# A state-space and MLP block in one kernel: the second tile's first norm moved ahead of the first tile's second norm, with another order at both ends

## The chip, the cores and the metric

The kernel runs on one core of one Trainium2 chip. The metric is the device time of one launch in microseconds (us), the median of several runs. A profile is one execution of the same program, taken by the hardware profiler; its span runs from the first to the last instruction of the program on the core, and its own time is a little longer than the span.

Engines are named as in the profile: PE (TensorE matmul), PEld (its weight loads), DVE (VectorE), ACT (ScalarE), POOL (GpSimd) and SP (SyncE, which here only issues DMAs). Each engine takes its instructions in the order of the program.

## What is computed

The input `u` has 16 sequences of 1024 steps with 256 channels; `c` has one conditioning row for each sequence. Everything is float32. Cut to what matters, with `mod` split into six rows of 256 for each sequence:

```python
mod = (silu(c) @ wmod).reshape(16, 6, 1, 256)
sa, ca, ga, sb, cb, gb = (mod[:, i] for i in range(6))
ga, gb = sign(ga) * maximum(abs(ga), 0.25), sign(gb) * maximum(abs(gb), 0.25)

h  = layernorm(x) * (1 + ca) + sa              # first norm, "a"
Bu = (h @ W_B.T + b_B) * exp(log_dt)
xs = scan(state = A_bar * state + Bu)          # along the sequence
x  = x + ga * (xs @ W_C.T + b_C + h @ W_D.T + b_D)

h  = layernorm(x) * (1 + cb) + sb              # second norm, "b"
y  = square(relu(h @ W_fc.T)) @ W_proj.T       # 256 -> 1024 -> 256
x  = x + gb * (spikes of y in 5 steps) / 5
```

The number of spikes depends on `y` alone and rises at five levels, so the kernel counts how many levels `y` exceeds.

## The kernel before

**Tiles.** The 16 x 1024 rows are cut into 32 tiles of 512 rows (`TILES`, `TT`); tiles 2b and 2b+1 are the two halves of sequence b, and the scan of an odd tile goes on from the state of the even one. A tile lies in SBUF either with channels on the partitions (two blocks of 128, `KD`) and 512 rows along the free dimension, or with rows on the partitions (four blocks of 128, `SUB`), which is where a norm's moments are taken.

**Products.** A float32 value is split into a high part (rounded to the matmul's fp32r form, by an ACT copy) and a low part (the rest, by a DVE subtraction), and every product is made in three passes: high by high, low weight by high value, high weight by low value (`PASSES`, line 222). So a block of 128 x 128 x 512 costs three matmuls, and every operand needs an ACT step (`..._hi`, `halves`) and a DVE or POOL step (`..._lo`, `halves_lo`).

**One tile's way.** Its names in the profile:

- `moments`, `aggregate`, `root_in_v`, `root`, `newton_v` (lines 243 to 305): the first norm's statistics on DVE (tiles st_a, mv_a, v_a), a square root on ACT (q_a), then five small DVE steps to the scale and the shift (r_a, m_a). `normalise` or `normalise_by` (lines 307 to 328) apply them (xn_a), on ACT alone or on the engines listed.
- To bring xn_a to channels on the partitions the first tiles use `transpose` (line 384: eight 128 x 128 transposes on PE into pt_a), all later ones `hop` (line 330): a 32 x 32 transpose on DVE (w_a), four DMAs to DRAM (hop_a) and one back (v_a). `scaled_hi`/`scaled_lo`, or `turned_hi`/`turned_lo` after a hop, multiply by 1 + ca and split: h_a.
- `state_input` (line 408): 12 matmuls with W_B into pb. `state_bias` on ACT (bu), `state_scan` on DVE (xs), `state_hi`/`state_lo` (xsp).
- `mix_h` (line 445): 12 matmuls of h_a with W_D into py; `mix_xs` (line 450): 12 of xsp with W_C into the same py. `mix_out` or `mix_out_late` make x1 (in the profile x or x_N), the residual stream; with `mix_out` the input tile x has had a constant added by `residual` before.
- The second norm, the same with b for a, from xm: `transpose_back` (line 395: eight transposes on PE into pm) for tiles 0 and 1, `hop_back` (line 344, hop_x, xm) later.
- `expand` (lines 478 to 503), for each of four pairs of hidden blocks: 12 matmuls into pf, then on ACT relu (a), square (a) and the high copy (hid); `hidden_lo` makes the low half. `contract` (line 516): 12 matmuls for each pair into pp.
- `spike` (line 524): five DVE comparisons (o); `gated` on ACT, `output` on POOL, then the DMA out.

**Order.** The order on each engine is that of the program text: `InOrder` (line 71) keeps it. From tile 2 on `period(t)` (line 871) interleaves the expand and contract steps of tile t with the first norm of tile t+4, the scan of t+3, the mix of t+2 and the second norm of t+1. `first_period` (line 718) and `second_period` (line 821) are written out by hand, as is the front (lines 614 to 716), where modulations, weights and the first tile's chain are made, and `last_tile` (line 548), which works in column halves of 256 rows. `load` and `load_q` (lines 110 to 123) fetch x and xq.

**Buffers that matter.** PSUM: `ps_f` has four buffers, `ps_y` and `ps_p` two each (lines 99 to 101); SBUF: tag "hid" four, "relu" three, "o" four. The raw weights wm1, wm2, ff and fp lie in "hid" buffers until they have been used.

**Small products.** `columns` (line 206) makes one modulation row for all sequences (ps_sa, ps_ca, ps_ga, ps_cb, ps_sb, ps_gb), ps_bb, ps_bd and ps_bf the biases that follow from them. They are float32 matmuls with 16 columns; each is two instructions in the profile. `run_idle` (line 618) multiplies zeros while the first inputs are on their way.

Of the kernel before, what the change touches and what calls it, by code (L numbers as in the profile page):

```python
# [21 lines left out]
F32 = mybir.dt.float32  # L22
# [64 lines left out]
def adaln_kernel(ctx: ExitStack, tc: tile.TileContext, x, xq, w_bT, w_cT, w_dT, w_fcT, w_projT, cols,  # L87
# [38 lines left out]
    Q.dma_start(out=col, in_=cols)  # L126
# [6 lines left out]
    load_q(0)  # L133
    Q.dma_start(out=wm1[:, :, 0:D], in_=wm_v[:, :, 0:D])
    fb, fcm, fd = (work.tile([P, KD, D], F32, tag="relu", name=n, bufs=3) for n in ("fb", "fc", "fd"))
    Q.dma_start(out=fb, in_=w_bT.rearrange("(k p) n -> p k n", p=P))
    Q.dma_start(out=wm1[:, :, D:2 * D], in_=wm_v[:, :, D:2 * D])
# [327 lines left out]
    def residual(t):  # L465

        b = t // 2
        for m in range(KD):
            G.tensor_scalar(xts[t][:, m], xts[t][:, m], gac[:, m, b:b + 1], None, ALU.add)
# [78 lines left out]
    def last_tile(t):  # L548
# [4 lines left out]
        hid = [work.tile([P, 2, 2, TT], F32R, tag="hid", name=f"hid_{t}_{pair}", bufs=HIDB)  # L553
               for pair in range(KF // 2)]

        def expand_half(g, pair):
            a = work.tile([P, 2, half], F32, tag="relu", name=f"a_{t}_{pair}_{g}", bufs=3)
# [9 lines left out]

        acc = ps_p.tile([P, KD, half], F32, tag="ps_p", name=f"pp_{t}_0")
        for pair in range(KF // 2):
            expand_half(0, pair)  # L570
            if pair < 2:
                output(t - 2, (pair, 0))
# [17 lines left out]
        for m, pairs in ((0, (0, 1)), (1, (0, 1)), (0, (2, 3)), (1, (2, 3))):  # L590
# [27 lines left out]
    def run_idle(n):  # L618
        PE.matmul(ps_zero[:, 0:n], lhsT=zero[:, 0:P], rhs=zero[:, 0:n], start=True, stop=True)

    for _ in range(2):
        run_idle(TT)
    silu_c()
    S.activation(sa[:, 0, 0:1], edt, AF.Sqrt)
    ps_sa = columns(wm1, 0, "sa")
    decay(6)
# [3 lines left out]
    root("a0")  # L630
    S.activation(sa, ps_sa, AF.Copy)
    decay(1)
    ps_ca = columns(wm1, 1, "ca")
# [6 lines left out]
    S.activation(wb[:, 0], fb, AF.Identity, scale=edt)  # L640
    S.activation(wd[:, 0], fd, AF.Copy)
    newton_v("a0", lambda: decay(1))
    normalise_by("a0", blocks_of(xqs[0]), (V, S, V, S))
    V.tensor_scalar(s1, ps_ca, 1.0, None, ALU.add)
    V.scalar_tensor_tensor(wb[:, 1], fb, edt, wb[:, 0].bitcast(F32), ALU.mult, ALU.subtract)
    transpose("a0")
    decay(2)
# [3 lines left out]
    scaled_hi("a0", lambda k: pts["a0", k])  # L651
    scaled_lo("a0", lambda k: pts["a0", k])
    V.tensor_tensor(wd[:, 1], fd, wd[:, 0].bitcast(F32), ALU.subtract)
    S.activation(wc[:, 0], fcm, AF.Copy)
    state_input(0)
# [11 lines left out]
    state_scan(0, (1,))  # L667
    state_lo(0, slice(0, 1))
    V.tensor_tensor(wc[:, 1], fcm, wc[:, 0].bitcast(F32), ALU.subtract)
    state_hi(0, slice(1, 2))  # L670
# [4 lines left out]
    state_lo(0, slice(1, 2))  # L675
    mix_xs(0)
    ps_cb = columns(wm2, 1, "cb")
    ps_sb = columns(wm2, 0, "sb")
    mix_out_late(0)
    S.activation(sb, ps_sb, AF.Copy)  # L680
    moments("a1", blocks_of(xqs[1]))
    transpose_back(0, ps_p, "ps_p")
    moments("b0", xms[0])
    aggregate("b0")
    root_in_v("b0")
    root("b0")
    halves(wf, ff, *fc(0))
    newton_v("b0")
    V.tensor_scalar(s2, ps_cb, 1.0, None, ALU.add)
    normalise_by("b0", xms[0], (V, S, V, S))  # L690
    halves_lo(wf, ff, *fc(0), V)
    clipped(columns(wm2, 2, "gb"), gb, sil, 1.0 / STEPS)

    ps_bf = ps_f.tile([P, KF, NB], F32, tag="ps_f", name="ps_bf")

    def shift_f(*blocks):
        for m in blocks:
            for k in range(KD):
                PE.matmul(ps_bf[:, m], lhsT=ff[:, k, m * P:(m + 1) * P], rhs=sb[:, k],
                          start=k == 0, stop=k == KD - 1)  # L700

    shift_f(0, 1, 2, 3, 4, 5, 6)
    transpose("b0")
    shift_f(7)
    halves(wf, ff, *fc(1))
    halves_lo(wf, ff, *fc(1), G)
    scaled_hi("b0", lambda k: pts["b0", k])
# [163 lines left out]
    def period(t):  # L871
# [17 lines left out]
        if one:  # L889
            root(b1)  # L890
# [97 lines left out]
```

## Time and profile before

| | us |
|---|---|
| median of 3 runs | 1006.14 (1005.83 to 1007.24) |
| the profiled execution, its own time | 1003.88 |
| its span | 1002.1 |
| first matmul (zeros) | 1.44 |
| first matmul of tile 0 with 512 columns (pb) | 11.99 |
| first matmul of tile 0's expand (pf) | 34.29 |
| end of the last mix_h in `first_period` | 83.63 |
| end of the last matmul | 995.2 |
| end of the last DVE instruction | 998.81 |

Landing times of the first DMAs, from the DMA view: col (issued by SP at 0.72) 2.46, xq of tile 0 (issued at 1.17) 4.82, the first third of wm1 5.51, fb 6.81, the second third of wm1 7.55, fd 8.29, fc 9.73, xq of tile 1 11.01, wm2 14.24, ff 16.81, fp 22.32.

How to read it: a row of a timeline has the start, the time from the start of the first to the end of the last merged instruction, the engine, the line (all have that of the recording helper, 81, so one goes by tiles), the operation with out<-in, and the number of instructions; in brackets the idle time before and what ended it. Matmuls are pipelined, and one that waits for an operand is shown as busy; whether PE flows is seen from the steps between starts.

### The profile page before, as it was taken

How to read it: one execution, taken by the hardware profiler on the slowest of the kernel's cores; microseconds unless marked ns; L12 is line 12 of the kernel's file. 1: busy time of each engine (PE TensorE's matmuls, PEld its weight loads, DVE VectorE, ACT ScalarE, POOL GpSimd, SP SyncE). 2: the span in 40 equal slices, each digit the busy share in tenths (PEclk: the TensorE clock that was granted, in tenths of full speed). 3: DMA queues.
4: the chain of work that ended last, by engine and by line, in shares of the span. 5: the costliest groups of instructions: out<-in, count | busy, mean ns of one | idle time of the engine just before them, and what ended most of it. 6: DMA issues, size and time to landing. Idle time of an engine off the chain costs nothing.

```text
span 1002.1 us, 13540 instructions
## 1 busy us (share of the span) xinstructions
PE 989.8 (99%) x4468; PEld 819.7 (82%) x4468; DVE 856.0 (85%) x1654; ACT 767.4 (77%) x1157; POOL 288.7 (29%) x317
## 2 busy tenths in 40 slices
PE   8999999999999999999999999999999999999997
PEld 6877778888888888888888888888888888888887
DVE  6788998898888899888889888889888889887775
ACT  4676888778778878777878777878777877876785
POOL 0202232332332232332232332233332233332111
PEclk8899999999999999999999999999999999999999
DMA  7134455555544555545555544554554554453321
GB/s 284 49 121 147 147 155 167 166 154 164 182 133 151 180 157 155 172 140 152 171 163 154 168 136 153 174 168 148 168 152 143 168 168 148 147 161 112 99 70 43
DMA packets 125335, 150.09 MB, mean 150 GB/s; under 512 B 9552, under 2 KB 89424, under 8 KB 125264
## 3 DMA queue, kind: packets, MB, share of 16 engines
q1 hardware_dynamic: 125264, 149.22, 48.7%
q8 instruction: 35, 0.57, 0.2%
q14 instruction: 36, 0.29, 0.1%
HBM read 85.22 MB, written 63.96 MB: 149 GB/s over the span
## 4 chain that ended last, share of the span: by engine, by line
PE 84%; DVE 4%; DMA 2%; ACT 1%; issue 1%; SPq 0%; DVEq 0%
PE pp L81 31%; PE pf L81 31%; PE py L81 15%; PE pb L81 7%; DVE o L81 2%; DMA v_b<-hop_b 1%; DMA hop_b<-w_b 0%; DVE st_b L81 0%; DMA v_a<-hop_a 0%; SPq L81 0%; DVE w_b L81 0%; DVE hid L81 0%; ACT xn_a L81 0%; ACT a L81 0%; ACT h_b L81 0%
## 5 line engine op out<-in xcount | busy, mean ns | idle before, releaser
L81 PE MATMUL pp<-hid,wp 128*128 128x512 f32 (+1 forms) x1584 | 366.9, 383 | 2.0 <-DVE o L81 0.7
L81 PE MATMUL pf<-h_b,wf 128*128 128x512 f32 (+1 forms) x1584 | 365.5, 383 | 0.0
L81 PEld LDWEIGHTS pp<-hid,wp 128*128 128x128 f32 x1584 | 290.3, 188 | 63.4 <-DVE hid L81 2.4
L81 PEld LDWEIGHTS pf<-h_b,wf 128*128 128x128 f32 x1584 | 291.7, 188 | 58.5 <-DVE h_b L81 0.4
L81 ACT ACTIVATE a<-pf,bias_f 128x512 f32<-128x512 f32 (+1 forms) x264 | 169.1, 668 | 156.4 <-PE pf L81 156.2
L81 DVE TENSOR_TENSOR hid<-a,hid 128x1024 fp32r<-128x1024 f32 (+1 forms) x131 | 152.1, 1181 | 93.0 <-ACT hid L81 93.0
L81 POOL TENSOR_TENSOR o<-o,x 128x512 f32<-128x512 f32 x64 | 108.2, 1710 | 298.0 <-ACT o L81 298.0
L81 DVE SCALAR_TENSOR_TENSOR o<-pp,o 128x512 f32<-128x512 f32 (+1 forms) x260 | 177.4, 682 | 7.9
L81 ACT ACTIVATE a<-a 128x1024 f32<-128x1024 f32 (+1 forms) x132 | 136.7, 1036 | 4.2
L81 ACT ACTIVATE hid<-a 128x1024 fp32r<-128x1024 f32 (+1 forms) x132 | 136.7, 1035 | 4.2
L81 POOL TENSOR_SCALAR x<-x,gac 128x512 f32<-128x512 f32 x60 | 93.5, 1568 | 29.2 <-DVE o L81 19.9
L81 POOL TENSOR_SCALAR v_a<-mv_a 128x4 f32<-128x4 f32 x26 | 15.6, 600 | 283.6 <-DVE mv_a L81 283.6
L81 PE MATMUL pb<-h_a,wb 128*128 128x512 f32 x384 | 94.3, 394 | 0.1
L81 PE MATMUL py<-xsp,wc 128*128 128x512 f32 x384 | 92.7, 390 | 0.5 <-ACT xsp L81 0.5
L81 PE MATMUL py<-h_a,wd 128*128 128x512 f32 x384 | 92.4, 389 | 0.0
L81 PEld LDWEIGHTS pb<-h_a,wb 128*128 128x128 f32 x384 | 73.0, 190 | 16.5 <-ACT h_a L81 0.9
L81 PEld LDWEIGHTS py<-xsp,wc 128*128 128x128 f32 x384 | 71.9, 188 | 15.9 <-ACT xsp L81 1.1
L81 PEld LDWEIGHTS py<-h_a,wd 128*128 128x128 f32 x384 | 72.0, 188 | 15.0
L81 ACT ACTIVATE xn_a<-xq,m_a,r_a 128x256 f32<-128x256 f32 x124 | 64.3, 592 | 1.6 <-PE pb L81 1.1
L81 ACT ACTIVATE xn_b<-xm,m_b,r_b 128x256 f32<-128x256 f32 x120 | 61.9, 587 | 1.0 <-DVE m_b L81 1.0
L81 DVE TENSOR_SCALAR o<-pp 128x512 f32<-128x512 f32 (+1 forms) x65 | 44.4, 682 | 13.3 <-PE pp L81 13.1
L81 ACT ACTIVATE o<-o,gb 128x512 f32<-128x512 f32 (+1 forms) x65 | 42.6, 702 | 3.5 <-issue 3.5
(123 smaller groups left out, 839.4 us busy)
## 6 DMA issues: line engine op xcount, KB each, us to landing
xq<-in_xq SPq DMA_DIRECT2D x32, 512.0 KB, 6.7
x<-in_x SPq DMA_DIRECT2D x32, 512.0 KB, 5.1
out<-o SPq DMA_DIRECT2D x63, 256.0 KB, 6.8
hop_a<-w_a SPq DMA_DIRECT2D x120, 128.0 KB, 2.5
v_a<-hop_a SPq DMA_DIRECT2D x30, 512.0 KB, 4.0
hop_x<-w_x SPq DMA_DIRECT2D x120, 128.0 KB, 3.1
xm<-hop_x SPq DMA_DIRECT2D x30, 512.0 KB, 3.2
hop_b<-w_b SPq DMA_DIRECT2D x120, 128.0 KB, 2.5
```

The source lines that it names most:

```text
L81: return self.tc.keep_in_program_order(issue(*args, **kwargs))
```

## The change

The diff touches four places.

1. **Loads.** col is issued by ACT's queue in place of SP's; xq of tile 0 goes first on SP, in two halves; the thirds of wm1 change places (ca's columns before sa's).
2. **Front.** `run_idle` now multiplies zeros in fp32r form, twelve times at first and three times after each of ps_ca and ps_sa. Tile 0's transposes come ahead of ps_bb; the high copy of wd comes after h_a. Tile 1's first norm (moments, aggregate, root, newton, normalise), its transposes, h_a and its W_B products (`state_input(1)`) come ahead of tile 0's second norm. ps_bf is made in two halves, the second one and ps_gb only after tile 0's first expand products, and ps_bf moves to the pool ps_y. The steps of `first_period` stand in another order (tile 1's second norm ahead of tile 3's normalise, among others), and `residual(2)` is done by ACT.
3. **The last periods.** `period` runs to tile 29; in tile 29 newton stands before the second spike, normalise and hop before the next steps, `turned_hi`/`turned_lo` before the last expand, and the last contract is left to the next period. Tile 30 has a period of its own, `period_before_last`.
4. **The last tile.** Its first expand products stand ahead of contract(30, 3), the spikes of tile 30 stand between them, and the last contract runs in another order of pairs.

```diff
-    Q.dma_start(out=col, in_=cols)
+    S.dma_start(out=col, in_=cols)
+    xqs[0] = io.tile([P, SUB, D], F32, tag="xq", name="xq_0", bufs=2)
+    for s in (slice(0, 2), slice(2, 4)):
+        Q.dma_start(out=xqs[0][:, s], in_=xq[0][:, s])
...
-    def residual(t):
+    def residual(t, E=G):
...
+            if E is S:
+                S.activation(xts[t][:, m], xts[t][:, m], AF.Identity, bias=gac[:, m, b:b + 1])
+            else:
+                G.tensor_scalar(xts[t][:, m], xts[t][:, m], gac[:, m, b:b + 1], None, ALU.add)
...
     def last_tile(t):
...
+        expand_half(0, 0)
+        expand_half(0, 1)
+        contract(t - 1, 3)
+        for m in range(KD):
+            output(t - 2, (m, 0))
+        for m in range(KD):
+            spike(t - 1, accs.pop((t - 1, m)), (m, 0))
+            expand_half(0, 2 + m)
         acc = ps_p.tile([P, KD, half], F32, tag="ps_p", name=f"pp_{t}_0")
-        for pair in range(KF // 2):
-            expand_half(0, pair)
-            if pair < 2:
-                output(t - 2, (pair, 0))
...
-        for m, pairs in ((0, (0, 1)), (1, (0, 1)), (0, (2, 3)), (1, (2, 3))):
+        for m, pairs in ((0, (0, 1, 2)), (1, (0,)), (0, (3,)), (1, (1, 2, 3))):
...
     def run_idle(n):
-        PE.matmul(ps_zero[:, 0:n], lhsT=zero[:, 0:P], rhs=zero[:, 0:n], start=True, stop=True)
-
-    for _ in range(2):
-        run_idle(TT)
+        for _ in range(n):
+            PE.matmul(ps_zero, lhsT=zero[:, 0:P].bitcast(F32R), rhs=zero.bitcast(F32R), start=True, stop=True)
+
+    run_idle(12)
     silu_c()
     S.activation(sa[:, 0, 0:1], edt, AF.Sqrt)
+    ps_ca = columns(wm1, 1, "ca")
+    run_idle(3)
     ps_sa = columns(wm1, 0, "sa")
+    run_idle(3)
```

The front from tile 0's statistics on, as it reads after the change (small steps left out):

```python
    normalise_by("a0", blocks_of(xqs[0]), (V, S, V, S))
    S.activation(sa, ps_sa, AF.Copy)
    ...
    transpose("a0")
    decay(4)
    ...
    scaled_hi("a0", lambda k: pts["a0", k])
    scaled_lo("a0", lambda k: pts["a0", k])
    ...
    moments("a1", blocks_of(xqs[1]))
    state_input(0)
    state_bias(0)
    state_scan(0, (0,))
    mix_h(0)
    ...
    state_hi(0, slice(0, 1))
    state_scan(0, (1,))
    aggregate("a1")
    root_in_v("a1")
    root("a1")
    state_hi(0, slice(1, 2))
    V.tensor_tensor(wc[:, 1], fcm, wc[:, 0].bitcast(F32), ALU.subtract)
    state_lo(0, slice(0, 1))
    newton_v("a1")
    state_lo(0, slice(1, 2))
    normalise_by("a1", blocks_of(xqs[1]), (S, S, V, S))
    clipped(ps_ga, ga, gac, 1.0)
    ...
    mix_xs(0)
    transpose("a1")
    ps_cb = columns(wm2, 1, "cb")
    ps_sb = columns(wm2, 0, "sb")
    mix_out_late(0)
    V.tensor_scalar(s2, ps_cb, 1.0, None, ALU.add)
    scaled_hi("a1", lambda k: pts["a1", k])
    S.activation(sb, ps_sb, AF.Copy)
    transpose_back(0, ps_p, "ps_p")
    scaled_lo("a1", lambda k: pts["a1", k])
    moments("b0", xms[0])
    aggregate("b0")
    root_in_v("b0")
    state_input(1)
    state_bias(1, (0,))
    root("b0")
    halves(wf, ff, *fc(0))
    state_bias(1, (1,))
    newton_v("b0")
    normalise_by("b0", xms[0], (V, S, V, S))
    halves_lo(wf, ff, *fc(0), V)
    shift_f(0, 1, 2, 3)
    transpose("b0")
    ...
```

`first_period` after, up to where it reads as before again (three dots mark steps left out):

```python
        r0 = expand_begin(0, 0)
        ...
        r0(0)
        root("a2")
        halves(wf, ff, *fc(2))
        state_scan(1)
        newton_v("a2")
        shift_f(4, 5, 6, 7)
        r0(1)
        halves_lo(wf, ff, *fc(2), V)
        clipped(columns(wm2, 2, "gb"), gb, sil, 1.0 / STEPS)
        residual(2, S)
        r1 = expand_begin(0, 1)
        normalise_by("a2", blocks_of(xqs[2]), (S, V, S, V))
        hop("a2")
        load_q(4)
        r1(0)
        mix_h(1)
        state_hi(1)
        state_lo(1)
        r0(2)
        hidden_lo(0, 0)
        ...
        mix_xs(1)
        r2(0)
        root("a3")
        mix_out_late(1)
        contract(0, 0)
        newton_v("a3")
        turned_hi("a2")
        turned_lo("a2")
        r2(1)
        transpose_back(1, ps_f, "ps_f")
        ...
        r2(2)
        root("b1")
        halves(wf, ff, *fc(3))
        newton_v("b1")
        halves_lo(wf, ff, *fc(3), V)
        contract(0, 1)
        normalise("a3", blocks_of(xqs[3]))
        hop("a3")
        load_q(5)
        state_input(2)
        state_bias(2)
        state_scan(2)
        normalise("b1", xms[1])
        ...
        hidden_lo(0, 2)
        mix_h(2)
        ...
        turned_hi("a3")
        turned_lo("a3")
        r3 = expand_begin(0, 3)
        ...
```

The period of tile 30 (t = 30), new:

```python
    def period_before_last(t):
        b1 = f"b{t + 1}"
        rest = expand_begin(t, 0)
        rest(0)
        ...
        contract(t - 1, 3)
        rest(1)
        normalise(b1, xms[t + 1])
        rest(2)
        spike(t - 1, accs.pop((t - 1, 0)), (0, 0))
        hop(b1)
        for m in range(KD):
            output(t - 2, (m, 0))
        expand(t, 1)
        spike(t - 1, accs.pop((t - 1, 1)), (1, 0))
        hidden_lo(t, 0)
        expand(t, 2)
        hidden_lo(t, 1)
        rest = expand_begin(t, 3)
        rest(0)
        hidden_lo(t, 2)
        rest(1)
        contract(t, 0)
        rest(2)
        contract(t, 1)
        turned_hi(b1)
        turned_lo(b1)
        ...
        hidden_lo(t, 3)
        contract(t, 2)
```

## The prediction

> **What bounds the kernel now.** I read the page first, then the busy time by stretch, then the timelines of PE, DVE and ACT at both ends, and last the step from each matmul's start to the next. PE sets the end, so what counts is where its stream has holes.
>
> ```profile
> PE 989.8 (99%) x4468; PEld 819.7 (82%) x4468; DVE 856.0 (85%) x1654; ACT 767.4 (77%) x1157; POOL 288.7 (29%) x317
> ```
>
> The 99% hides the holes, because a matmul that waits for its operand counts as busy. The steady step shows them: two successive groups of the middle, twelve products of 512 columns each, start 2.72 us apart, 0.227 us per product.
>
> ```profile
> 912.74 2.88 PE L81 MATMUL pb<-h_a,wb 128*128 128x512 f32 x12
> 915.46 2.88 PE L81 MATMUL pp<-hid,wp 128*128 128x512 f32 x12
> ```
>
> Against 0.227 (0.121 for 256 columns, 0.101 for the instructions of small products and transposes) the stream loses 12.5 us from 0 to 36, 2.7 from 36 to 92, 1.9 from 92 to 150, nothing from 150 to 940, and 1.9 between 945 and 970. Only the ends can move.
>
> The stretches (us, then busy time of PE, PEld, DVE, ACT, POOL; granted TensorE clock; DMA) show the front's first cause: the clock is halved twice, once while tile 0's W_B products run and once into its first expand products.
>
> ```profile
> 8.80:15.60 6.80, 6.74 (x23) 5.38 (x24) 4.22 (x13) 3.24 (x7) 0.00 (x0) 0.51 1.03 411
> 15.60:29.30 13.70, 13.70 (x95) 12.47 (x93) 9.85 (x27) 4.40 (x10) 0.00 (x0) 0.99 0.44 158
> 29.30:36.10 6.80, 6.80 (x30) 6.54 (x31) 5.18 (x20) 4.00 (x8) 2.27 (x2) 0.51 0.00 0
> 150.00:940.00 790.00, 790.00 (x3487) 654.36 (x3486) 692.06 (x1288) 620.94 (x920) 249.90 (x280) 1.00 0.52 155
> ```
>
> PE's timeline shows the chain: pb takes 4.68 us instead of 2.72, the eight transposes before it 1.9 instead of 0.8, and from x1 (pm, 25.68) to the first pf (34.29) PE has small products alone.
>
> ```profile
> 10.11 1.95 PE L81 MATMUL pt_a<-ident,xn_a 128*128 128x128 f32 x8
> 11.99 4.84 PE L81 MATMUL pb<-h_a,wb 128*128 128x512 f32 x12
> 16.67 2.90 PE L81 MATMUL py<-h_a,wd 128*128 128x512 f32 x12
> ...
> 21.11 3.03 PE L81 MATMUL py<-xsp,wc 128*128 128x512 f32 x12
> ...
> 25.68 1.07 PE L81 MATMUL pm<-ident,x 128*128 128x128 f32 x8
> ...
> 31.84 1.95 PE L81 MATMUL pt_b<-ident,xn_b 128*128 128x128 f32 x8
> ...
> 34.29 4.01 PE L81 MATMUL pf<-h_b,wf 128*128 128x512 f32 x13
> ```
>
> DVE there: a1's moments stand ahead of b0's.
>
> ```profile
> 24.54 1.36 DVE L81 TENSOR_TENSOR x<-x,x 128x512 f32<-128x512 f32 x2 [1.91 <-ACT x L81]
> 25.81 1.40 DVE L81 BATCH_NORM_STATS2 st_a<-xq 128x6 f32<-128x256 f32 x4
> 27.13 1.41 DVE L81 BATCH_NORM_STATS2 st_b<-pm 128x6 f32<-128x256 f32 x4
> ```
>
> At the end PE's last group starts at 989.29 and stops at 995.2. DVE counts spikes of column half m=0 from 993.87 for 2.2 us, so m=1 starts at 996.05, 0.75 us after PE is done.
>
> ```profile
> 993.87 0.43 DVE L81 TENSOR_SCALAR o<-pp 128x256 f32<-128x256 f32 x1 [1.24 <-PE pp L81]
> ...
> 996.05 0.41 DVE L81 TENSOR_SCALAR o<-pp 128x256 f32<-128x256 f32 x1
> ...
> 998.33 0.48 DVE L81 SCALAR_TENSOR_TENSOR o<-o,gb,x 128x256 f32<-128x256 f32 x1
> ```
>
> **Base of the sum.** The profiled execution took 1003.88 us (span 1002.1 and 1.8 around it), 2.26 below the median 1006.14; I take the saving off the median.
>
> **Tile 0's first norm.** col leaves by ACT's queue, xq0 first on SP in two halves. SP issued xq at 1.17 and it landed at 4.82; now it is issued at 0.72 and should land by 4.4, but DVE is at its decay steps until 4.67, so moments gain only 0.2. col (landed 2.46, then ACT's exp at 2.49) is issued at the same 0.7, now beside xq0's packets and ahead of ACT's table load (1.28): between no loss and 0.5, and I take 0.1, because ACT's wait for it was 0.49 after a table load that now ends 0.4 later. On PE, 12 zero products at some 0.43 us under half clock (the two fp32 ones now take 3.78 us for four instructions, also half speed) run from 1.44 until about 6.0, under the cover of the wait for wm1 (landed 5.5); two times three more (0.7 us each) stand between ca and sa, and PE is free for the transposes at 9.05. xn is ready at 9.3 (ACT no longer copies wd ahead of it, 0.55), the transposes end at 9.9 at full clock, the first high half of h_a at 10.4 (was 11.9), bb behind the transposes holds PE until 10.7. pb then ends at 13.6, not 16.67: lo of h_a, wd lo and bias_b (0.75+0.75+0.6+0.5) run on DVE meanwhile.
>
> **Second tile's norm ahead.** a1's moments (1.40) now stand before the scans: these run 14.65 to 17.05 (were 16.10 to 18.81). Then aggregate 0.4, v 0.2 and the root, 0.2. The root waits on ACT for v until 17.7, and queued behind it is the second xsp copy (to 18.5), for which PE waits 0.5; newton (1.0) stands on DVE between the two xsp lo's, the second ending at 20.25. py<-xsp runs 17.9 to 21.0, 2.9 earlier. Most is given back: ACT does three xn_a blocks (0.55 each) and the |ga| before x1, which starts at 22.75 (was 23.72); DVE adds end at 24.9 (25.9), then s2 and h_a1 lo (1.5) stand before b0's moments: 26.45 (was 27.13). The same steps as now to xn_b, transposes at full clock (0.8 for 1.55): first pf at 32.0; with pb1 under half clock, which holds ACT's second bu and PE some 0.8 longer, 32.8. Taken: 32.4, 1.9 earlier.
>
> **Work moved across that point.** pb1 and a1's transposes come before it (2.72+0.81), half of ps_bf and ps_gb go behind (1.62+0.81): 1.1 us less is left.
>
> **First period.** After pf starts I count 44.85 us of PE work to the end of mix_h(3), and holes of 1.75: 0.4 for the low half of h_b, 0.25 before pm, 0.35 at contract(0,2) (hidden_lo behind the xn_b copies and wp halves), 0.6 at contract(0,3), small ones. residual(2) moves from POOL to ACT (1.25, beside pf_2) and wf lo of fc(2) from POOL (1.28) to DVE (0.65, beside ps_bf); both are in the count. SP's queue is free by then: load(2) goes first, then hop a2's five issues (0.4 each) and load_q(4) as now; v_a2 should land 7.6 after w_a's transpose (it ended at 48.41, v_a landed at 56.05), 1.8 before ACT asks for it. Half clock after the first pf: 0 if the stretch stays full, 1.7 if a 3.4 us window halves; taken 0.8, as now. So mix_h(3) ends at 32.4+46.6+0.8=79.8 against 83.63: front gain 3.8. Bounds: 1.3 (holes and half clock twice as long, 2.55 more) to 5.9 (full clock, half the holes, pf at 32.0). DVE ends state_lo(3) 6.1 us after mix_h(3), now 5.9, so the 1.9 lost in the second period stays.
>
> [...] The rows: in 25.9 to 29.3 PE was busy without pause, yet with small products and transposes alone, and the next row is half clock. [...]
>
> **Tail.** contract(29,3) moves behind pf of tile 30 and contract(30,3) behind two half-width pf pairs, which covers the three holes (0.5, 0.7, 0.5 and small steps, 1.9). New ones: the root of b31 waits on ACT for xm_31 (landed 950.8; I get 949.8), so tile 30's third pair waits 0.8 for its PSUM buffers; contract(30,0) waits 1.0 for spike(29,1), now behind the hop's transpose; 0.3 at contract(29,3). Sum -0.2. SP sees hop b31 before output(28), which costs nothing: only the copies out are behind. The new order of late leaves 18 products (18x0.121=2.2 us) after m=0 completes, the length of its spikes, so m=1 starts when PE ends: 0.75. hid lo of pair 3 (was ready 992.63) is then needed at 992.7. Tail gain 0.5, bounds -1.6 (the named holes twice, 2.1 more) and 2.6 (none).
>
> **Sum.** 3.8+0.5=4.3: 1001.8 us.
>
> **Rivals.**
> 1. The queues of DVE and ACT eat it: DVE is busy 38.6 of 47.9 us from 36 to 84, so an earlier PE only waits more; only the moved work is kept, 1.1: 1005.1. Against: DVE starts earlier too.
> 2. Slower: a serial chain in the first period. xn_a of tile 3 now stands on ACT behind x1(1) and the root of b1; before it stood ahead of that root:
>
> ```profile
> 57.82 1.42 ACT L81 ACTIVATE x<-py,gac,ga 128x512 f32<-128x512 f32 x2
> ...
> 61.73 2.08 ACT L81 ACTIVATE xn_a<-xq,m_a,r_a 128x256 f32<-128x256 f32 x4 [0.51 <-DVE m_a L81]
> ...
> 72.89 1.34 ACT L81 ACTIVATE h_a<-v_a,s 128x512 fp32r<-128x512 f32 x2 [1.20 <-DMA v_a<-hop_a]
> ```
>
> From w_a (63.95) to h_a it takes 8.9; behind h_a stand pf_6's relus, hid_3 and contract(0,3). Each us by which x1(1) starts later than 17.8 after the first pf costs one. Eight late (pf+26; now it is pf+23.5) gives 1009.8; it is slower than before from 6.3.
> 3. Half clock in both fill stretches (PE has no 512-column product in 21.0 to 25.4 and 28.1 to 32.0): 0.4 on pf's start and 0.9 on the products: 1003.1. [...]
> 4. Full clock throughout (0.4+0.8) and no new hole in the tail (1.5): 999.1.
> That the change does not do what it says is out: the built order of PE's instructions has a1's transposes and pb1 before b0's.
>
> **How the numbers follow.** Forecast 0.47; rival 1 0.16, 2 0.08, 3 0.15, 4 0.14. A measurement tells 0.2% (2 us) from no change: faster (under 1004.1) is the forecast, 3, 4 and a little of 1, 0.74; same 0.17; slower rival 2 and a rest, 0.09. Range 998.4 to 1005.6: it holds all but rival 2, the far part of 1, and the low end of 4.
>
> **What would show it.** The first pf near 32.4; pb under full clock near 11 to 13.6; py<-xsp near 18; mix_h(3) ending near 80; the step sum from 150 to 940 still nil; the last spike starting within 0.1 of PE's end. The prediction is wrong if pf starts after 33.5, if holes from pf to 92 exceed 4 us, or if 940 to the end loses more than 3.5 us.

## The result, and the profile after

| | before | after |
|---|---|---|
| median, us | 1005.99 (1004.58 to 1007.24, 6 runs) | 999.26 (998.58 to 1000.21, 6 runs) |
| profiled execution, us | 1003.88 | 999.28 |
| span | 1002.1 | 997.5 |

The ratio is 0.9935, 95% interval 0.9922 to 0.9948: faster by 6.7 us in the medians, 4.6 in the two profiled executions. Why these two are not the same is the main question below. (One execution of the kernel before, in a later session, took 1243.74 us at a mean granted clock of 0.747; it stands in no ratio here.)

The stretches of the profile after (columns as before: us, busy time of PE, PEld, DVE, ACT, POOL, granted clock, DMA):

```profile
8.80:15.60 6.80, 6.46 (x36) 5.10 (x36) 6.54 (x27) 4.88 (x10) 0.00 (x0) 1.00 1.03 410
15.60:29.30 13.70, 13.47 (x86) 11.73 (x84) 11.33 (x38) 6.86 (x16) 0.00 (x0) 1.00 0.69 234
29.30:36.10 6.80, 6.46 (x30) 4.67 (x30) 5.58 (x19) 3.96 (x8) 1.28 (x1) 0.75 0.00 0
150.00:940.00 790.00, 790.00 (x3486) 654.36 (x3485) 689.13 (x1274) 617.91 (x916) 248.82 (x279) 1.00 0.52 155
```

The first stretch has the full clock (0.51 before), and the third has it half of the time (0.75 for 0.51): the record of the granted clock has two half-clock stretches of 6.83 before, 8.62 to 15.45 and 29.10 to 35.93, and one of 3.41 after, 32.24 to 35.66. PE's timeline there:

```profile
9.99 1.35 PE L81 MATMUL pt_a<-ident,xn_a 128*128 128x128 f32 x8 [0.32 <-DVE xn_a L81]
...
11.99 3.07 PE L81 MATMUL pb<-h_a,wb 128*128 128x512 f32 x12
14.90 2.89 PE L81 MATMUL py<-h_a,wd 128*128 128x512 f32 x12
...
19.33 3.03 PE L81 MATMUL py<-xsp,wc 128*128 128x512 f32 x12
...
26.23 2.98 PE L81 MATMUL pb<-h_a,wb 128*128 128x512 f32 x12
29.05 1.85 PE L81 MATMUL ps_bf<-sb,ff 128*128 128x16 f32 x16
...
33.02 4.41 PE L81 MATMUL pf<-h_b,wf 128*128 128x512 f32 x12
```

pb of tile 0 starts where it did (11.99) but is through in 2.91 instead of 4.68, the step to py. The first pf starts 1.27 earlier (34.29 before), with tile 1's transposes and pb already behind it. It takes 4.24 to the next group where 2.72 is the steady step: the half-clock stretch lies on it, and its second product waits for h_b.

Tile 0's norm starts late because of col, which ACT waits for:

```profile
3.89 0.23 ACT L81 ACTIVATE sil<-col 128x32 f32<-128x32 f32 x1 [1.45 <-DMA col<-in_cols]
```

Issued at the same 0.72, col now lands at 3.87 instead of 2.46, beside the halves of xq (3.67 and 4.55), and so the decay steps and the moments behind them on DVE start later (moments at 6.00 for 4.85). Whether pb would start earlier without this is tried below.

The half of the change that gave the title, on DVE:

```profile
24.40 1.36 DVE L81 TENSOR_TENSOR x<-x,x 128x512 f32<-128x512 f32 x2 [0.91 <-ACT x L81]
25.68 0.18 DVE L81 TENSOR_SCALAR s<-ps_cb 128x32 f32<-128x32 f32 x1
25.78 1.40 DVE L81 SCALAR_TENSOR_TENSOR h_a<-pt_a,s,h_a 128x512 fp32r<-128x512 f32 x2
27.09 1.42 DVE L81 BATCH_NORM_STATS2 st_b<-pm 128x6 f32<-128x256 f32 x4
```

b0's moments start at 27.09, 27.13 before: h_a of tile 1 stands where a1's moments stood, so DVE's chain to b0 gained nothing. The gain is on PE, which does a1's transposes and pb there; before, all of ps_bf and ps_gb stood in that place.

From there on, an offset of 3.16 us that no longer changes from tile 5 on:

```profile
909.58 2.88 PE L81 MATMUL pb<-h_a,wb 128*128 128x512 f32 x12
```

(912.74 before.) At the end, DVE and PE:

```profile
985.34 6.05 PE L81 MATMUL pp<-hid,wp 128*128 128x256 f32 x48
...
989.33 0.42 DVE L81 TENSOR_SCALAR o<-pp 128x256 f32<-128x256 f32 x1 [0.65 <-PE pp L81]
...
991.51 0.41 DVE L81 TENSOR_SCALAR o<-pp 128x256 f32<-128x256 f32 x1
...
993.79 0.48 DVE L81 SCALAR_TENSOR_TENSOR o<-o,gb,x 128x256 f32<-128x256 f32 x1
```

PE ends at 991.38, and the spikes of m=1 start 0.13 later (0.84 before, by the same measure). The steps of PE's starts over their steady length add up as follows, in us:

| stretch | before | after |
|---|---|---|
| 0 to 36 | 12.5 | 7.6 |
| 36 to 92 | 2.7 | 1.6 |
| 92 to 150 | 1.9 | 1.6 |
| 150 to 940 | none | none |
| 940 to the end | 1.9 | 1.1 |

Zero products count as work in these sums, so the first row is not what the front gained: the first pf starts 1.27 earlier.

### The profile page after: what moved, and what is told of

It reads as the page before. It is cut to its first block, busy times and chain, and to the rows that moved or that the text cites. A ratio compares the mean times of both kernels' runs of the same rounds, so it can differ in the third digit from the quotient of the medians.

```text
span 997.5 us, 13570 instructions
## 1 busy us (share of the span) xinstructions
PE 987.3 (99%) x4482; PEld 818.6 (82%) x4482; DVE 859.6 (86%) x1657; ACT 767.5 (77%) x1158; POOL 285.7 (29%) x314
## 4 chain that ended last, share of the span: by engine, by line
PE 87%; DVE 3%; DMA 1%; ACT 1%; issue 1%; SPq 0%; DVEq 0%
PE pp L81 32%; PE pf L81 32%; PE py L81 16%; PE pb L81 7%; DVE o L81 1%; DMA v_a<-hop_a 0%; ACT a L81 0%; DMA v_b<-hop_b 0%; DVE hid L81 0%; DVE w_b L81 0%; DMA hop_b<-w_b 0%; ACT hid L81 0%; DVE x L81 0%; DVE st_b L81 0%; DVE st_a L81 0%
## 5 line engine op out<-in xcount | busy, mean ns | idle before, releaser
L81 DVE TENSOR_TENSOR hid<-a,hid 128x1024 fp32r<-128x1024 f32 (+1 forms) x131 | 154.2, 1197 | 83.8 <-ACT hid L81 83.8
L81 POOL TENSOR_SCALAR x<-x,gac 128x512 f32<-128x512 f32 x58 | 90.2, 1563 | 22.6 <-DVE o L81 22.6
L81 DVE SCALAR_TENSOR_TENSOR h_b<-v_b,s,h_b 128x512 fp32r<-128x512 f32 x60 | 41.8, 737 | 4.9 <-ACT h_b L81 4.9
```

The lines of the kernel that those rows point to most:

```text
L81: return self.tc.keep_in_program_order(issue(*args, **kwargs))
```

## The experiments

Medians are device us; "before" is the kernel before on the same chip in the same session (medians 1005.5 to 1006.1). PE's hole sums are worked out as in the table above.

### Front or tail, and how much one execution differs from the next

**The kernel before, unchanged, once more.**

> The kernel before, unchanged, to see why its profiled execution (1003.88) lies 2.1 us under the median of its runs (1005.99) while the changed kernel's profiled execution (999.28) lies on its median. Theory A: executions of the kernel before differ in how long the granted clock is halved in the front (the half-clock stretches are whole 3.4 us windows whose phase differs from one execution to the next), so runs with a lower mean clock are slower, and the spread is 1 to 3 us. Rival B: the runs differ at the same mean clock (loads, DMA). Ratio 1.000 in both.

Ratio 0.9998 (0.9989 to 1.0008), eleven times from 1004.24 to 1008.25. The profiled execution is the longest of them, with a span of 1006.5: 4.4 us more than the span of the first profile of the same program. PE's timeline, and the stretches:

```profile
8.79 1.89 PE L81 MATMUL ps_ca<-sil,wm 128*128 128x16 f32 x8 [1.23 <-DMA wm<-in_wmod]
...
12.23 1.95 PE L81 MATMUL pt_a<-ident,xn_a 128*128 128x128 f32 x8
14.10 4.48 PE L81 MATMUL pb<-h_a,wb 128*128 128x512 f32 x12
```

```profile
29.30:36.10 6.80, 6.80 (x39) 6.80 (x38) 4.65 (x21) 3.21 (x8) 1.27 (x1) 0.58 0.00 0
36.10:40.60 4.50, 4.50 (x13) 3.70 (x13) 3.91 (x16) 1.93 (x4) 1.28 (x1) 0.50 0.00 0
```

Everything up to pb runs at half speed (eight small products 1.89, at full clock 0.96 or 1.04): here the clock became full only at 16.76, in the first profile at 5.21, for 3.41. And the second half-clock stretch is 10.24 long instead of 6.83, 30.42 to 40.66.

Not all of the 4.4 is the clock. The second third of wm1, issued at the same time (2.62 and 2.61), landed at 8.75 here and at 7.55 in the first profile, and ps_ca waits for it. Its row in the first profile:

```profile
7.59 1.06 PE L81 MATMUL ps_ca<-sil,wm 128*128 128x16 f32 x8 [0.92 <-DMA wm<-in_wmod]
```

Followed from matmul to matmul, PE is 1.20 later at ps_ca, and half clock over ps_ca makes this 2.01 at ps_bb. The extra 3.41 of half clock over the first pf products brings 1.2 more, and waits between 50 and 130 us, whose cause was not looked for, another 1.2 (1.20 and 0.8 and 1.2 and 1.2 make the 4.4). So theory A and rival B each hold in part. That slower executions have a lower mean clock, as theory A asks, the times do not show: three at 0.991 took 1004.24 to 1004.77, four at 0.995 took 1004.67 to 1006.02. This mean cannot decide, as it counts the start as full clock until the first record (last section). The first profile of before, 1003.88, lies below all eleven times: it was a lucky execution, in the clock and in that load.

**Front alone**: loads, zeros, front and first period of the change, with the last periods and the last tile of before.

```diff
-    def period_before_last(t):
...
-        for m, pairs in ((0, (0, 1, 2)), (1, (0,)), (0, (3,)), (1, (1, 2, 3))):
+        for m, pairs in ((0, (0, 1)), (1, (0, 1)), (0, (2, 3)), (1, (2, 3))):
```

> The changed front and first period, with the old last periods and the old last tile. The profiles give the front 3.2 us (steady groups start 3.16 us earlier). Theory A: the further 2.1 us by which the medians differ is clock in the front, so this kernel is 5.3 us faster than before (1000.7). Rival B: it is 3.2 us faster (1002.8) and the rest sits in the tail.

1002.37 (999.61 to 1004.24), ratio 0.9959 (0.9944 to 0.9973): 3.7 us under before, nearer to rival B (1002.8) than to theory A (1000.7). Its eight times lie in two groups, three at 999.61 to 999.81 and five at 1002.05 to 1004.24, with one and the same front. In the profiled execution (1003.65, of the upper group) the clock halves twice, 33.83 to 37.24 and 40.66 to 44.07:

```profile
36.10:40.60 4.50, 4.50 (x31) 4.08 (x31) 4.08 (x10) 2.88 (x5) 0.00 (x0) 0.87 0.02 4
40.60:44.10 3.50, 3.50 (x10) 2.71 (x10) 2.14 (x6) 3.09 (x6) 0.00 (x0) 0.51 0.01 2
```

The stretch before the second one, 37.24 to 40.66, held the second half of ps_bf and ps_gb (37.86 to 40.46):

```profile
37.86 1.85 PE L81 MATMUL ps_bf<-sb,ff 128*128 128x16 f32 x16
39.56 1.04 PE L81 MATMUL ps_gb<-sil,wm 128*128 128x16 f32 x8
40.46 4.58 PE L81 MATMUL pf<-h_b,wf 128*128 128x512 f32 x12
```

PE was busy throughout it, yet with 16-column products alone for three quarters of it.

**Tail alone**: the front of before with the changed end, that is, the same lines taken into the kernel before.

```diff
+    def period_before_last(t):
...
-        for m, pairs in ((0, (0, 1)), (1, (0, 1)), (0, (2, 3)), (1, (2, 3))):
+        for m, pairs in ((0, (0, 1, 2)), (1, (0,)), (0, (3,)), (1, (1, 2, 3))):
```

> The old front and first period, with the new last periods and the new last tile. The profiles give the tail 1.4 us (0.7 of holes, 0.7 after the last matmul). Theory A: 1.4 us faster than before (1004.6). Rival B: 3.5 us faster (1002.5).

1004.74 (1003.1 to 1005.76), ratio 0.9983 (0.9974 to 0.9991); holes from 940 on 1.06. This is theory A's 1.4. The two parts multiply to 0.9959 x 0.9983 = 0.9942, inside the interval of the whole change (0.9922 to 0.9948); in medians they make 3.7 and 1.35 of the 6.7. The six times of the changed kernel (998.58 to 1000.21) hold none like the upper group of front alone, so some of the 6.7 may be luck on its side too.

**col back on SP's queue, first.**

```diff
-    S.dma_start(out=col, in_=cols)
+    Q.dma_start(out=col, in_=cols)
```

> The changed kernel with col issued first on SP again, xq of tile 0 behind it in two halves. In the changed kernel col landed at 3.87 (2.46 before) and tile 0's moments began at 6.00 (4.85 before). Theory: col's few small packets share the engines with xq's and come late; with col first on SP it lands near 2.5, moments begin near 4.9, but PE's queue (zero products to 9.4) lets the transposes start only 0.5 us earlier, so the first pf comes 0.3 to 0.5 us earlier and the time is 998.8. Rival: the late start is carried in full, and the time falls by 1.1 to 998.1. Second rival: it was hidden, no difference.

1000.45 (998.33 to 1001.43), ratio 0.9945 (0.9932 to 0.9959): no difference that these runs can tell. col landed at 2.38, but xq and wm behind it later (4.05, 4.84 and 6.92), and pb started at 12.00. The moments began at 4.51, but ps_ca waited for wm until 7.05, and with the zeros behind it PE came to the transposes at 10.32 only (9.99 in the changed kernel). So the late col cost nothing that moving it back would save.

### The parts of the front

**The zeros of before** in the changed kernel.

```diff
-    run_idle(12)
+    for _ in range(2):
+        PE.matmul(ps_zero, lhsT=zero[:, 0:P], rhs=zero, start=True, stop=True)
...
-    run_idle(3)
...
-    run_idle(3)
```

> The changed kernel with the zero products of the kernel before: two fp32 products of 512 columns at the start, none between ps_ca and ps_sa and none after ps_sa. Theory (the fp32r zeros are what kept the clock full over tile 0's transposes and W_B products): a half-clock stretch comes back between about 8.5 and 15.5, the eight transposes take 1.6 to 1.9 us instead of 1.35 and pb 4.2 to 4.8 instead of 2.91, everything behind it moves back by 1.5 to 2.3, the median by as much: 1000.8 to 1001.6 against 999.3. Rival (the order of the loads and of bb behind the transposes gave the full clock, the zeros nothing): pb within 0.3 of 2.91, median 999.0 to 999.7.

1001.49 (1000.09 to 1002.02), ratio 0.9948 (0.9937 to 0.996): 2.2 us more in the medians than with the new zeros, but the intervals of the two ratios overlap, and the profiled executions (1000.50 and 999.28) differ by 1.2. A half-clock stretch came back as the theory says, but not quite at its place: the clock is half from the start up to 16.74.

```profile
7.16 1.87 PE L81 MATMUL ps_sa<-sil,wm 128*128 128x16 f32 x8
10.07 1.94 PE L81 MATMUL pt_a<-ident,xn_a 128*128 128x128 f32 x8 [1.04 <-DVE xn_a L81]
...
13.37 4.56 PE L81 MATMUL pb<-h_a,wb 128*128 128x512 f32 x12
```

From 16.74 on the clock then stays full, also over the first pf products: they start 2.04 later (35.06) but take 3.22 to the next group, where the changed kernel's half-clock stretch makes it 4.24. So half of the loss comes back in this execution.

Over all profiles with these zeros: with two fp32 products (four instructions, over by 5.2) the clock became full at 5.21, 5.4, 16.74 and 16.76; with twelve fp32r ones (until 5.8 to 6.9) at 4.28 to 7.63 in all nine. So with the old zeros the clock was full before 6 in two profiles of four only.

**The middle of before**: the titular move undone, and with it the halves of ps_bf, the place of ps_gb and the order of the first period; loads, zeros and tail kept.

```diff
-    moments("a1", blocks_of(xqs[1]))
     state_input(0)
...
-    transpose("a1")
...
-    state_input(1)
...
     def first_period():
...
+        transpose("a1", ps_p, "ps_p")
...
+        state_input(1)
```

> The changed kernel with the middle of the kernel before: tile 1's norm, transposes and W_B products behind tile 0's second norm again, all of ps_bf and ps_gb ahead of the first pf, the old first period; loads, zeros, tile 0's first norm, last periods and last tile stay changed. Theory (the move fills PE ahead of the first pf: 1.1 us of work changes sides and the half-clock stretch gets shorter): half clock over at least 6.8 us somewhere between 27 and 38, first pf no earlier than 32.0, the last mix_h of the first period 1.4 to 3 us later than 80.74, median 1000.7 to 1002.3. Rival (the front's gain is tile 0's norm at full clock alone, and DVE and ACT take back what the move gives): mix_h ends within 0.5 of 80.74 and the median is 999.0 to 999.8.

1002.54 (1001.4 to 1003.1), ratio 0.9961 (0.9949 to 0.9973): 3.3 us more. The first pf starts at 33.35, 0.33 later only, but after 4 us of small products and transposes alone the clock is half for 10.24, 26.48 to 36.72, and the two first pairs take 7.15 from 33.35 to 40.50 instead of 5.44:

```profile
25.66 5.40 PE L81 MATMUL ps_bf<-sb,ff 128*128 128x16 f32 x28
...
33.35 7.30 PE L81 MATMUL pf<-h_b,wf 128*128 128x512 f32 x24
```

28 instructions of ps_bf take 5.40 here, 16 in the changed kernel 1.85. What the norm's move does and what the shorter rows of small products do was not separated. In the medians the zeros and this middle, 2.2 and 3.3, make 5.5, which is what lies between tail alone (1004.74) and the whole change (999.26); front alone, measured directly, gave 3.7, and the front's gain is known no closer than that.

### Can the last half-clock window be closed?

**warm**: zero products in unused columns of ps_bf's bank, four ahead of tile 0's second transposes and two behind.

```diff
     shift_f(0, 1, 2, 3)
+    keep_warm(4)
     transpose("b0")
+    keep_warm(2)
```

> The changed kernel with six more zero products (fp32r, 384 columns, into unused columns of ps_bf's bank): four ahead of tile 0's second transposes and two behind them, while PE waits for xn_b and h_b. Theory (the half-clock window over the first pf comes from 3.4 us with small products and transposes alone): the window from 32 to 36 is full, pf's twelve products take 2.7 to 3.3 instead of 4.24, pf starts no later than 33.2, median 1.0 to 1.5 lower, 997.8 to 998.3. Rival (zeros there only move the window to the stretch of ps_bf and ps_gb behind pf, or the window is set by something else): one half-clock window stays between 28 and 44, median 998.9 to 999.6.

1002.41 (1001.96 to 1002.92), ratio 0.9961: 3 us slower than the changed kernel, which neither theory had.

```profile
32.07 1.65 PE L81 MATMUL ps_bf<-zero 128*128 128x384 f32 x4 [1.11 <-DVE bias_f L81]
```

The zeros write into the tile that DVE copies to bias_f, so they waited for that copy, and the transposes behind them started at 33.52 instead of 30.86. Two half-clock stretches are in this profile, 31.59 to 35.00 and 41.83 to 45.24, the first of them over that wait and the transposes. The experiment added a wait on PE's queue and so does not answer its question.

**best**: another front, the work of DVE partly on POOL.

```diff
-    V.tensor_tensor(wd[:, 1], fd, wd[:, 0].bitcast(F32), ALU.subtract)
+    G.tensor_tensor(wd[:, 1], fd, wd[:, 0].bitcast(F32), ALU.subtract)
```

wc, xsp and the first wf are treated in the same way, and tile 0's moments stand ahead of the decay steps; the other moves are those named in the expectation.

> The changed kernel with another front: tile 0's moments ahead of the decay steps, the low halves of wd, wc, xsp and the first wf by POOL, ga and gac ahead of tile 1's normalise, ps_cb ahead of tile 1's transposes, tile 0's second moments ahead of tile 1's low half of h_a, pb of tile 1 in two parts around three accumulated zero products and tile 0's second transposes, all of ps_bf behind the first pf. Theory (the front is now bound by DVE's queue, and PE has some 2.5 us of holes and 1.5 us of half clock left from 12 to 37): pb starts near 10.6, the first pf between 29.3 and 30.7, the first period ends 2.5 to 3.5 earlier than 80.74, median 995.7 to 996.8. Rival (the small products gathered at 20 to 26 bring half clock over pb of tile 1, or POOL's slower steps hold xsp): pf at 31.5 or later, median 998 to 999.5.

1003.81 (1001.87 to 1006.45), ratio 0.9982 (0.9971 to 0.9992), longer than either theory had; pf starts at 33.78, on the rival's side (31.5 or later). In the profiled execution, the fastest of the twelve, pb starts at 11.65, since s1 stood on DVE ahead of newton and waited 1.2 us for ps_ca, and then small DVE steps are long beside POOL's:

```profile
12.47 1.29 POOL L81 TENSOR_TENSOR wd<-fd,wd 128x512 fp32r<-128x512 f32 x1 [11.18 <-ACT wd L81]
...
13.05 2.17 DVE L81 SCALAR_TENSOR_TENSOR abar<-abar 128x2 f32<-128x2 f32 x3
13.72 1.29 POOL L81 TENSOR_TENSOR wc<-fc,wc 128x512 fp32r<-128x512 f32 x1
```

Three steps of two elements a partition take 2.17 (four take 0.74 at 10.84 in the changed kernel): more in the last section.

**warm2**: the zeros ahead of that copy, and the small groups behind pf spread.

```diff
+            if m in (1, 3):
+                keep_warm(3)
...
-        shift_f(4, 5, 6, 7)
...
         r1 = expand_begin(0, 1)
+        shift_f(4, 5, 6, 7)
```

> The changed kernel with three fp32r zero products of 384 columns behind blocks 0 and 1 of ps_bf and three behind blocks 2 and 3, all ahead of the copy of ps_bf, so that they wait for nothing (in the kernel warm they stood behind that copy and started 1.2 us late, with tile 0's transposes behind them); and with the second half of ps_bf behind the second pair's products and ps_gb behind the third pair's, so that no two small groups stand together after pf. Theory (a half-clock window follows a window of 3.41 us in which PE has little besides small products and transposes): no half clock from 12 to 100 us, pf's first twelve products in 2.7 to 3.3, the last mix_h of the first period ends at 78.8 to 79.8, median 997.2 to 998.4. Rival (zeros of two operands that hold nothing but zeros do not count for the clock at this place, or the phase of the windows alone decides): a half-clock window between 28 and 44 again, median 998.9 to 1000.5.

1001.0 (1000.64 to 1001.6), ratio 0.9955 (0.9941 to 0.9968). The clock followed the theory: no half clock from 7.63 to the end of PE's work. The time followed neither: 1.7 us slower than the changed kernel. The holes have moved behind pf, 4.4 from 36 to 100. PE and ACT there:

```profile
53.88 1.32 PE L81 MATMUL pm<-ident,x 128*128 128x128 f32 x8 [0.71 <-DVE x L81]
...
74.19 3.06 PE L81 MATMUL pb<-h_a,wb 128*128 128x512 f32 x12 [1.73 <-ACT a L81]
```

```profile
59.20 2.07 ACT L81 ACTIVATE xn_a<-xq,m_a,r_a 128x256 f32<-128x256 f32 x4
...
72.22 1.34 ACT L81 ACTIVATE h_a<-v_a,s 128x512 fp32r<-128x512 f32 x2 [5.83 <-DMA v_a<-hop_a]
```

pb of tile 3 comes 1.9 late. What releases it is ACT's first relu (a from pf, which ends near 74.15 and frees a PSUM buffer); this stands on ACT behind h_a, and h_a waits for v_a, which came through xn_a and the hop. In the changed kernel the same rows are:

```profile
58.11 2.06 ACT L81 ACTIVATE xn_a<-xq,m_a,r_a 128x256 f32<-128x256 f32 x4
...
70.03 1.34 ACT L81 ACTIVATE h_a<-v_a,s 128x512 fp32r<-128x512 f32 x2 [4.74 <-DMA v_a<-hop_a]
```

There the hole ahead of that pb is 0.27 only: the chain of tile 3's norm is just on time. In warm2 ps_gb's DVE steps stood ahead of a3's moments (50.31 for 49.23), xn_a came 1.1 later and v_a 2.2 later, at 72.2.

**best3**: warm2 with DVE and ACT reordered in the front, nothing on POOL, ten zeros at first.

```diff
-    run_idle(12)
+    run_idle(10)
...
-    normalise_by("a1", blocks_of(xqs[1]), (S, S, V, S))
...
     V.tensor_tensor(gac, gac, ga, ALU.mult)
+    normalise_by("a1", blocks_of(xqs[1]), (S, S, V, S))
```

> The kernel warm2 with three moves on DVE and ACT and none to POOL: tile 0's moments ahead of the decay steps (two blocks ahead of sil), ga and gac ahead of tile 1's normalise, ps_cb ahead of tile 1's transposes; ten zero products at first and none behind ps_sa. Theory (the front waits for DVE's queue, and the kernel best lost its gain to DVE steps that ran at half their speed beside POOL and to s1 waiting for ps_ca in front of everything): pb starts at 10.5 to 11.0, x1 on ACT at 21.0 to 22.0 (23.59), pf at 30.5 to 31.5 (33.02), median 1.5 to 2.5 below that of warm2, 995.0 to 996.8. Rival (DVE's queue is full up to the scans whatever the order, so an earlier pb only waits at py<-xsp): pf within 0.7 of 33.0, median within 0.7 of warm2's.

1003.57 (1000.22 to 1004.2), ratio 0.9972 (0.9961 to 0.9982). Its twelve times lie in two groups, three at 1000.2 to 1000.9 and nine at 1003.1 to 1004.2, and the profiled execution, of the upper one, became full only at 17.68: pb started at 13.73 and took 4.66. From py<-xsp to x1 it is 2.61 us instead of 4.26, so the reorder of gac did what it should, and the slow start hid it. That the lower group had the full clock from early on is a guess; no profile fell there.

### The tail, and a version that joins the findings

**The old order of the last pairs.**

```diff
-        for m, pairs in ((0, (0, 1, 2)), (1, (0,)), (0, (3,)), (1, (1, 2, 3))):
+        for m, pairs in ((0, (0, 1)), (1, (0, 1)), (0, (2, 3)), (1, (2, 3))):
```

> The changed kernel with the old order of the last pairs (m=0 pairs 0 and 1, m=1 pairs 0 and 1, m=0 pairs 2 and 3, m=1 pairs 2 and 3). Theory (the new order gives the spikes of column half m=0 the time in which PE makes the rest of m=1): from the last matmul to the last DVE instruction 3.6 instead of 2.9 us, the last spike starts 0.8 to 0.9 after PE's end instead of 0.13, PE's hole sum from 940 to the end 1.1 to 1.4, median 999.9 to 1000.3 where the changed kernel has 999.3. Rival (the time after the last matmul is set by the spikes and the way out alone): within 0.2 of 2.9.

1000.74 (999.55 to 1001.24), ratio 0.995 (0.9937 to 0.9963); in the medians not to be told from the change. In the profile it can be: PE ends at 992.33, and the last DVE rows are

```profile
993.16 0.41 DVE L81 TENSOR_SCALAR o<-pp 128x256 f32<-128x256 f32 x1
...
995.45 0.48 DVE L81 SCALAR_TENSOR_TENSOR o<-o,gb,x 128x256 f32<-128x256 f32 x1
```

so m=1 starts 0.83 after PE (0.13 in the changed kernel), and DVE ends 3.60 after PE instead of 2.9. The new order is worth 0.7.

**chain**: the zeros of warm2 with ps_gb left alone, and tile 3's norm pulled forward.

```diff
-        hidden_lo(0, 1)
         moments("a3", blocks_of(xqs[3]))
...
+        hidden_lo(0, 1)
...
         root("a3")
+        newton_v("a3")
         mix_out_late(1)
...
+        normalise("a3", blocks_of(xqs[3]))
         r2(1)
...
         root_in_v("b1")
+        hop("a3")
```

> The changed kernel with two things: zero products behind blocks 0 and 1 (three) and 2 and 3 (two) of ps_bf, ahead of its copy, as in warm2 but with the second half of ps_bf and ps_gb where the changed kernel has them; and tile 3's norm earlier in the first period: its moments ahead of the second pair's low half, newton ahead of x1 of tile 1, its normalise on ACT ahead of the third pair's square, its hop on DVE ahead of newton of b1. Theory (in warm2 the 1.3 us saved at pf were lost at the W_B products of tile 3, which waited for v_a: the chain moments a3, xn_a, hop, v_a is what is late next): no half clock over pf, v_a of tile 3 lands at 66 to 68 (near 70 in the changed kernel), no hole above 0.1 ahead of pb of tile 3, the last mix_h ends at 79.0 to 79.7 (80.74), median 997.3 to 998.5. Rival (another chain of DVE and ACT, such as b1's norm or h_b of tile 1, is as late as that one): the hole goes elsewhere before 92, mix_h ends at 80.4 or later, median 998.9 or more.

997.19 (995.7 to 997.26, 5 runs), ratio 0.9913 (0.99 to 0.9927): the fastest, each run below each of the changed kernel's. The times lie in two groups, 995.7 and 995.71 at a mean clock of 0.998, and three from 997.19 to 997.26 at 0.996 to 0.997; the profiled execution is of the lower group, so the profile is not that of the median. The third stretch, and ACT at tile 3's h_a:

```profile
29.30:36.10 6.80, 6.37 (x39) 5.36 (x39) 5.61 (x19) 4.54 (x8) 1.30 (x1) 1.00 0.00 0
```

```profile
64.43 1.34 ACT L81 ACTIVATE h_a<-v_a,s 128x512 fp32r<-128x512 f32 x2 [0.69 <-DMA v_a<-hop_a]
```

Full clock over pf, v_a 5.6 earlier, no hole ahead of pb of tile 3; the last mix_h ends at 78.97 (80.74). PE's holes from 36 to 92 are 0.4 (1.6), from 92 to 150 none (1.6). The zeros and the earlier norm were not run apart; warm2 has the full clock without the earlier norm, and its holes from 92 to 150 are 1.8.

## Why the prediction was right, and where it was not

**Direction and range** held: 999.26 lies in 998.4 to 1005.6, and none of the three signs of being wrong came (pf at 33.02, holes from pf to 92 of 3.1, holes from 940 on of 1.1). The sum of 4.3 is close to the 4.6 between the two profiled executions, and short of the 6.7 between the medians. That it is so close is luck in part: the front was put 0.6 too high and the tail 1.0 too low.

**The base of the sum** is the step that did not hold: "The profiled execution took 1003.88 us (span 1002.1 and 1.8 around it), 2.26 below the median 1006.14; I take the saving off the median." The saving of one execution of before is not that of the typical one. Two executions of before differ by 4.4 us of span, 1.2 of it from the landing of wm1, 2.0 from the half clock over ps_ca and the first pf, and 1.2 from waits without a known cause. The change takes part of the half clock away, and in the medians the front is worth 3.7 (front alone) to 5.5 (zeros and middle), where the two profiles allow 3.16. That the profiled execution lay 2.26 under its median could have been read as this.

**Tile 0's first norm** (pb to end at 13.6): pb had the full clock, but was through at 14.90, and py<-xsp started at 19.33 for 17.9. col was put at 0 to 0.5 late and came 1.4 late. The run with col on SP shows that pb does not start earlier with an early col either, so the miss of 1.3 has no single cause there: with it ps_ca waits for wm instead.

**Second tile's norm ahead**: pf at 33.02 for 32.4. b0's moments were to gain 0.7 and gained 0.04. The work moved across pf was as counted.

**First period**: 80.74 for 79.8, 0.6 of it from pf. The half clock was put at 0.8, between 0 and the 1.7 of a 3.4 us window; no row of before shows a half-clock stretch of that length (both are 6.83). The profile after has one of 3.41, and the row of pf gives 1.5 (4.24 less 2.72), part of it the wait for h_b. So at this mark the front gained 2.89 (83.63 to 80.74) for 3.8, and 0.27 more came in the second period; the term that was mis-sized is the start of pb.

**Tail**: 1.46 (4.62 of span less the 3.16) for 0.5. The hole of 0.8 at tile 30's third pair did not come (xm_31 landed at 944.66, six earlier than before, where I had one earlier); the wait of contract(30, 0) was 0.7 where 1.0 was counted; the last spikes gave 0.7, as said.

**Rival 1** did not hold: the holes from 36 to 92 shrank instead of growing. **Rival 2** did not come in the changed kernel, where its chain has 0.27 of hole, but it is what comes next: a slip of 1.1 on it made a hole of 1.9 in warm2, and in chain, where it is pulled forward, the hole is gone. **Rival 3** came for one of its two stretches (granted clock 1.00 in 15.60:29.30, 0.75 in 29.30:36.10). The second period's 1.9 "stays", I wrote; 1.6 stayed, and it went when chain pulled the norm of tile 3 forward, while full clock without that (warm2) left 1.8.

**Rival 4** (full clock throughout, no new hole in the tail) gave 999.1, within 0.2 of the measured 999.26, but its conditions did not come: a half-clock stretch (32.24 to 35.66) lies over pf, and contract(30, 0) waited 0.7. That its number fits is luck; it comes from the base, as the 7.0 that it saves would be 996.8 from the profiled 1003.88.

**The half-clock stretches** are 3.41 in the profile after, twice 6.83 in the first of before and 10.24 ahead of and over pf in its second, one, two and three times 3.41 to within 0.01; they do not start at the same time in two executions of before (29.10 and 30.42 for the one over pf). What the rows of before showed, small products and transposes alone from 25.9 to 29.3 with PE busy and half clock behind them, came again in front alone: PE was busy all through 37.24 to 40.66, mostly with 16-column products, and from 40.66 to 44.07 the clock was half.

## What to carry to other kernels

Where the granted clock changes inside a profile, profile the same kernel twice before sizing anything from one page, and count an edit that keeps the clock by what the clock costs in the median execution. Make fill work long (here twelve products of 512 columns gave the full clock by 7.63 in nine profiles of nine, two fp32 ones in two of four, and with ten it came at 17.68 in the one profile), put it where it waits for nothing (in warm it waited 1.11 for a copy, and the kernel was 3 slower), and break up rows of small products with it (in warm2 and chain the clock in 29.30:36.10 was then 1.00, 0.75 in the changed kernel). When PE starts earlier, look for the chain that was just on time: in warm2 the clock was full, but small steps moved ahead of the next norm made it late and the kernel 1.7 slower; chain left them in place and pulled that norm forward.

## What the runs showed of the hardware that was not expected

- Some small DVE steps were long while POOL worked. In best two steps of 0.16 took 0.72 and 1.21, and they end within 0.02 of the POOL subtractions beside them (13.76 and 15.01); moments beside another POOL step took their usual 0.41 each, while v_a, a step of four elements a partition at 20.46, took 0.75 instead of 0.17 and ended at 21.21, within 0.03 of two POOL steps (18.47 to 21.18). What sets the long steps apart no run shows.
- A small load issued at the same time by another queue was not first here: col (20.5 KB, issued at 0.72) landed at 3.87 beside xq's packets, where it had landed at 2.46 when it led its queue.
- The stretch view shows a clock of 1.00 where the profile has no record: before 16.76 in the second profile of before it reads 1.00, while eight small products took 1.89. The steps between starts tell the clock there.
- The same v_a load of tile 3 took 3.7 us from issue to landing in the kernel before, 4.6 in the changed kernel and 5.7 in warm2. Why was not tried.
